# Two blocks, attention with a mixture of experts behind it: where norms, latents and shared pieces stand in the order of the work

## The chip, the cores and the metric

One core of a Trainium2 chip runs the whole program. A core has a matmul engine (TensorE, PE in the profile; its weight loads are shown apart as PEld), a vector engine (VectorE, DVE), a scalar engine (ScalarE, ACT), a general engine (GpSimd, POOL) and a queue engine (SyncE, SP) that issues most of the DMAs. The engines run side by side; each takes its own instructions strictly in the order in which they stand in its queue and waits at a semaphore where an instruction needs something of another engine.

The metric is the time of one execution on the device in microseconds (us), the median of several runs. A second figure is the span of one profiled execution, from its first to its last instruction.

## The reference

Four layers with a residual connection and a layer norm after each: a linear recurrence in place of attention, a quantized gated feed-forward, an attention with latent (low-rank) queries and keys, and a mixture of experts. There are 16 x 256 = 4096 rows of 256 columns, all in fp32. The last two are cut to what matters here:

```python
# second attention, H=16 heads, S=256, causal
cq = rms_norm(x @ w_qa.T, q_a_ln_w)                 # 192 columns
q = (cq @ w_qb.T)                                   # nope 128 + rope 64 per head
ckv = x @ w_kva.T                                   # 64 latent + 64 rope columns
k_pe = rope(ckv[..., 64:]); ckv_l = rms_norm(ckv[..., :64], kv_a_ln_w)
kv = ckv_l @ w_kvb.T                                # k_nope, v per head
attn = softmax(causal(q_full @ k_full.T * 192**-0.5))
x = layernorm(x + (attn @ v) @ w_o.T)
# experts: 32 of them, 4 for each row, at most 160 rows each
topk_idx, topk_w = router(x)
Y = (silu(Xp @ W_gate) * (Xp @ W_up)) @ W_down      # Xp: the rows of each expert
out = zeros.at[slots_token].add(Y * slots_w)
shared = silu(x @ shared_gate.T) * (x @ shared_up.T) @ shared_down.T
x = layernorm(x + out + shared)
```

## The kernel before

The 4096 rows are worked in 8 blocks (b) of 512 rows; a tile holds 128 rows, so a block has 4 tiles (tt). The rows stay on chip in `xs[b]` the whole time. Four stages follow one another: the recurrence (to about 860 us), the feed-forward (to 1126), the second attention (to 1917), and routing, experts and combine (to the end). The change touches the last two.

**Order.** In the second attention the order of PE, DVE, ACT and POOL is the order in which the Python code names the instructions (`manual_schedule`, `engines` are these four). The same holds for the loop over the experts. In the combine only PE's order is written by hand; the compiler plans the rest with a model of time. DMA issues on SP are planned by the compiler throughout.

**Second attention.** The loop over `n` takes one pair of heads of one block in each step: `b, p = divmod(n, 8)`, 64 steps and two before and one behind them. Step n makes, in this order: scores, maxima and exponentials of the first head of pair n+1 (`heads[0]`, L1104, L1115, L1128); the division of the second head of pair n (`divide`, a reciprocal on DVE, L1139, and two products on POOL, L1141); the queries of pair n+2 on PE (L1068 and L1074, two PSUM tiles of tag m, of which there are three); `first_place`; the division of `heads[0]`; the transposes of pair n-1's probabilities for the first sequence and their copies to SBUF by ACT (`keys_first`, a_ps L1154, aT L1158); the turns of the queries of pair n+2 (`turn`, six DVE instructions L1083 to L1085 and two POOL adds L1086); the scores of the second head, `heads[1]`; the contexts of the first sequence (c_ps, L1167, which wait for the copies aT); the transposes and copies for the second sequence; the maxima of `heads[1]`; `second_place`; the exponentials of `heads[1]`; the contexts of the second sequence. Up to three of POOL's row scatters (L1000) of an older block stand in between. The scores have two PSUM buffers (s_ps), which the maxima free.

`first_place` and `second_place` put other work into the steps. `moments` and `normalize` are a block's layer norm: at p = 2 of block b, DVE takes the moments of block b-1 behind its last output projection (o_ps, L1186) and POOL the power -1/2; at p = 3 `first_place` issues one small DVE instruction (shift, L159) and four ACT activations (L162), one for each tile. `step_route` advances the routing of block b-1 (mostly DVE, from p = 3 of block b to p = 1 of the next).

`latents(b)` is a generator of nine pieces that prepare the low-rank queries and keys of a block: the transposed rows (1), four times a product with `w_lat` on PE (lat_ps, L680), its copy and two squares on ACT, the last of them with the rms factors (DVE, then two powers on POOL; 2 to 5), eight scaled ACT copies cq (L704, L705; 6), the key columns kf on DVE (7), the transposed queries cqT (PE and ACT; 8), the transposed keys kT (9). For block b+1 they come at p = 7 of block b-1, then at p = 0, 1, 2, 3, twice in the two places of p = 4 (cq in `first_place`), once more in `second_place` of p = 4, and at p = 5. For block 1 the first piece comes ahead of the loop, the others in the steps of block 0 like all others.

**Experts and combine.** For each of 32 experts, PE transposes its rows (t_ps), multiplies gate and up (gu_ps, L1443) and down (d_ps, L1458); ACT scales the result (ye), and POOL issues two indirect stores of it to `res_d` in DRAM (L1472). `shared_pieces` is a generator of 40 pieces for the shared expert: transposed rows, two halves of gate and up with their silu, two halves of down with their addition to `xs`. 26 of them come ahead of the experts, one behind every eighth turn of the experts' loop (L1496, 4 in all), the last ten in the combine. The combine reads `res_d` back in 16 loads of 1 MB (L1528, nine buffers), each held back until all indirect stores have landed; for each load POOL adds two of the four rows of a token and `xs` (L1536), PE adds the others into PSUM with an identity matrix (y_ps, L1540), DVE adds the two sums (L1547), and behind each second load come moments, power, normalization on ACT (os, L162) and the store of 512 rows (L1514). Behind each load's matmuls `next(parts_, None)` puts one shared piece, and all that are left ahead of the last block.

Of the kernel before, what the change touches and what calls it, by code (L numbers as in the profile page):

```python
# [88 lines left out]
def seq_postln_kernel(ctx: ExitStack, tc: tile.TileContext, a: dict, out: bass.AP, cap: int):  # L89
# [54 lines left out]
    def moments(ys):  # L144

        n = len(ys)
        mv = small.tile([P, n, 2], F32, tag=f"mv{n}", name="mv")
        for i, y in enumerate(ys):
            st = small.tile([P, 6], F32, tag="bn", name="bn")
            nc.vector.bn_stats(st, y)  # L150
            nc.vector.bn_aggr(mv[:, i, :], st)
        rstd = small.tile([P, n], F32, tag=f"rstd{n}", name="rstd")
        rsqrt(rstd, mv[:, :, 1], 1.0, LN_EPS)
        return mv, rstd

    def normalize(ys, dsts, mv, rstd, eng=nc.vector):
        if eng is nc.scalar:
            shift = small.tile([P, len(ys)], F32, tag=f"shift{len(ys)}", name="shift")
            nc.vector.scalar_tensor_tensor(shift, mv[:, :, 0], -1.0, rstd, ALU.mult, ALU.mult)  # L159
        for i, (y, dst) in enumerate(zip(ys, dsts)):  # L160
            if eng is nc.scalar:
                nc.scalar.activation(  # L162
                    dst, y, AF.Identity, bias=shift[:, i : i + 1], scale=rstd[:, i : i + 1]
                )
            else:
                nc.vector.tensor_scalar(
                    dst, y, mv[:, i, 0:1], rstd[:, i : i + 1], ALU.subtract, ALU.mult
                )
# [123 lines left out]
    with ExitStack() as ph:  # L292
# [268 lines left out]
        with tc.manual_schedule(engines=engines):  # L561
# [7 lines left out]
            for m in range(NM + 1):  # L569
                b, p = divmod(m, NPR)  # L570
# [35 lines left out]
                if new:  # L606
# [5 lines left out]
                    if p in (3, 4, 5) and b + 1 < NB:  # L612
                        if p == 3:
                            mixing, xms_next = mixed(xb, nc.gpsimd, nc.gpsimd), {}
                        n, xm = next(mixing)
# [128 lines left out]
    with ExitStack() as ph:  # L744
# [35 lines left out]
        with ExitStack() as ff:  # L780
# [50 lines left out]
            last = None  # L831
            xT = transposed(0, mo_x, ps_t, "t")
            for b in range(NB):
# [9 lines left out]
                last = (b, hT)  # L843
# [30 lines left out]
        return x.unsqueeze(1).to_broadcast([P, K, GT, E])  # L874

    ROUTE_PARTS = 11
    ROUTE_PIECES, PIECES_EARLY, PIECES_STEP = 10, 14, 8
    SH_EARLY = 0
    xTs, dests, scattered = {}, {}, []

# [165 lines left out]
    with ExitStack() as ph:  # L1046
# [101 lines left out]
        def keys_first(heads, s):  # L1148

            aTs = []  # L1150
            for sm in heads:
                a_ps = ps_a.tile([P, 3 * P], F32, tag="a", name="a_ps")
                for i in range(3):
                    nc.tensor.transpose(  # L1154
                        a_ps[:, i * P : (i + 1) * P], sm.pr[:, s, i * P : (i + 1) * P], ident
                    )
                aT = pa.tile([P, 3 * P], F32, tag="aT", name="aT")
                copy = nc.scalar.copy(aT, a_ps)  # L1158
                aTs.append(aT)
            return aTs, copy  # L1160
# [38 lines left out]
        lats, routes, norms, sh_hTs = {}, {}, {}, {}  # L1199
# [8 lines left out]
        def step_latents(b):  # L1208
            if b < NB:
                if b not in lats:  # L1210
                    lats[b] = latents(b, ps_m, "m")
                next(lats[b])

        def step_route(b):
            if b >= 0:
                if b not in routes:
                    routes[b] = route(b, ps_m, "m")
                next(routes[b], None)

        def first_place(b, p):  # L1220
            last = b - 1
            if p == 3 and last >= 0:
                x = x_t[last * NTT : (last + 1) * NTT]
                normalize(x, x, *norms.pop(last), eng=nc.scalar)
            if p == 4:
                step_latents(b + 1)
            if p >= 5:
                step_route(last)
            if p == 0:
                step_route(last - 1)  # L1230

        def second_place(b, p):
            last = b - 1
            if p < 2:
                step_route(last - 1)
            if 3 <= p:
                step_route(last)
            if p == 4:
                step_latents(b + 1)
            if p <= 5 or p == 7:  # L1240
                step_latents(b + 2 if p == 7 else b + 1)
            if p in (1, 2) and last >= 0:
                output(last, 1, p - 1)
                if p == 2:
                    norms[last] = moments(x_t[last * NTT : (last + 1) * NTT])
            if p in (5, 6):
                output(b, 0, p - 5)
            if p == 7:
                shared(last, 0)
            if p == 0:  # L1250
                shared(last - 2, 3)
                shared(last - 1, 1)
            if p == 6:
                shared(last - 1, 2)

        def scatters(b, p):

            lo = 3 * (p - 2)
            return [(b, j) for j in range(max(lo, 0), min(lo + 3, GT * K))] if b >= 0 else []

        NS = NB * NP
        with tc.manual_schedule(engines=engines):
            qTs, sms = {}, {}
            step_latents(1)
            for n in range(-2, NS + 1):
                b, p = divmod(n, NP)
                todo = scatters(b - 2, p)

                def one_scatter():
                    if todo:  # L1270
                        scatter(todo[0][0], [todo.pop(0)[1]])

                scored = n + 1 if 0 <= n + 1 < NS else None
                asked = n + 2 if 0 <= n + 2 < NS else None
                seen = n - 1 if 0 <= n - 1 < NS else None
                if scored is not None:
                    kT = latent[scored // NP][2]
                    heads = sms[scored] = [Softmax(), Softmax()]
                    qT2 = qTs.pop(scored)
                    for s in range(2):  # L1280
                        heads[0].scores(qT2[0], kT, s)
                        heads[0].maxima(s)
                        heads[0].exps(s)
                if n in sms:
                    sms[n][1].divide()
                if asked is not None:
                    q_ps = queries(latent[asked // NP][0], asked % NP)
                if n >= 0:
                    first_place(b, p)
                if scored is not None:  # L1290
                    heads[0].divide()
                if seen is not None:
                    pair = sms.pop(seen)
                    kf = latent[seen // NP][1]
                    part, j = divmod(seen % NP, NP // 2)
                    if j == 0:
                        cT = cTs[seen // NP, part] = pc.tile(
                            [P, NP // 2, BLK], F32, tag="cT", name="cT"
                        )
                    c_ps = ps_c.tile([P, 2, S], F32, tag="c", name="c_ps")  # L1300
                    aTs0 = keys_first(pair, 0)
                if asked is not None:
                    qTs[asked] = [turn(ps, 2 * asked + k) for k, ps in enumerate(q_ps)]
                one_scatter()
                if scored is not None:
                    heads[1].scores(qT2[1], kT, 0)
                    heads[1].scores(qT2[1], kT, 1)
                if seen is not None:
                    contexts(c_ps, *aTs0, kf, 0)
                    aTs1 = keys_first(pair, 1)  # L1310
                if scored is not None:
                    heads[1].maxima(0)
                    heads[1].maxima(1)
                one_scatter()
                if n >= 0:
                    second_place(b, p)
                if scored is not None:
                    heads[1].exps(0)
                    heads[1].exps(1)
                if seen is not None:  # L1320
                    contexts(c_ps, *aTs1, kf, 1)
                    nc.scalar.copy(cT[:, j, :], c_ps.rearrange("p s t -> p (s t)"))
                one_scatter()
            step_route(NB - 2)
            last = NB - 1
            for s in range(2):
                output(last, 1, s)
            x = x_t[last * NTT :]
            layernorm(x, x)
# [26 lines left out]
    with ExitStack() as ph:  # L1356
        ps_t = ph.enter_context(tc.tile_pool(name="ps_t3", bufs=8, space=PSUM))
        sh_psum = ps_t, "t"
        parts_ = shared_pieces()
# [24 lines left out]
    with ExitStack() as ph:  # L1384
# [101 lines left out]
        with tc.manual_schedule(engines=engines):  # L1486
            now = {}
            for n in range(E + 2):
                if n < E:
                    now[n] = Expert(n)  # L1490
                    now[n].turned()
                if 0 <= n - 1 < E:
                    now[n - 1].hidden()
                if 0 <= n - 2:
                    now.pop(n - 2).result()
                if n % PIECES_STEP == PIECES_STEP - 1:  # L1496
                    next(parts_)
    exp.close()

    with ExitStack() as ph:
# [15 lines left out]
        for b in range(NB):  # L1518
# [6 lines left out]
            for pair in range(H):  # L1525
# [8 lines left out]
                n = K - 1 if b == NB - 1 else K - 2  # L1534
# [90 lines left out]
```

## Time and profile before

| | |
|---|---|
| time, median of three runs | 2145.63 us (2143.16 to 2147.37) |
| the profiled execution | 2142.17 us |
| its span | 2140.4 us |
| mean granted PE clock | 0.994 |
| busy PE / DVE / ACT / POOL | 2055.8 / 1560.8 / 763.0 / 899.4 us |
| DMA moved | 169.73 MB, 79 GB/s on average |

By stage (us from the start; busy us of each engine, from windows over the trace):

| stretch | what | PE | DVE | ACT | POOL | DMA share |
|---|---|---|---|---|---|---|
| 0 to 860 | recurrence | 843.3 | 721.9 | 167.0 | 260.7 | 0.44 |
| 860 to 1126 | feed-forward | 266.0 | 74.1 | 54.9 | 11.6 | 0.08 |
| 1126 to 1917 | second attention | 747.8 | 643.9 | 465.0 | 490.3 | 0.03 |
| 1917 to 1981 | routing of the last block, shared pieces | 61.5 | 35.3 | 17.6 | 32.5 | 0.30 |
| 1981 to 2063 | experts | 81.6 | 46.5 | 37.0 | 54.1 | 0.43 |
| 2063 to 2140 | last stores and combine | 55.7 | 39.1 | 21.5 | 50.2 | 0.73 |

How to read it: busy is the time in which an engine worked on an instruction; DMA share is how busy the 16 DMA engines were on average. A timeline line gives start, duration, engine, line, operation, output and inputs by their names in the program, shapes and the number of instructions merged; in brackets stand the idle time of the engine before it and what ended it. The chain of work that ended last is followed back from the last instruction: at each step to what released it, or to the instruction before it on the same engine.

### The profile page before, as it was taken

How to read it: one execution, taken by the hardware profiler on the slowest of the kernel's cores; microseconds unless marked ns; L12 is line 12 of the kernel's file. 1: busy time of each engine (PE TensorE's matmuls, PEld its weight loads, DVE VectorE, ACT ScalarE, POOL GpSimd, SP SyncE). 2: the span in 40 equal slices, each digit the busy share in tenths (PEclk: the TensorE clock that was granted, in tenths of full speed). 3: DMA queues.
4: the chain of work that ended last, by engine and by line, in shares of the span. 5: the costliest groups of instructions: out<-in, count | busy, mean ns of one | idle time of the engine just before them, and what ended most of it. 6: DMA issues, size and time to landing. Idle time of an engine off the chain costs nothing.

```text
span 2140.4 us, 29554 instructions
## 1 busy us (share of the span) xinstructions
PE 2055.8 (96%) x9544; PEld 1439.3 (67%) x9544; DVE 1560.8 (73%) x3960; ACT 763.0 (36%) x2237; POOL 899.4 (42%) x972
## 2 busy tenths in 40 slices
PE   8999999999999999999998999999999999989978
PEld 5777777777777777556564666666666666666866
DVE  7888888888888888232327669797978888875546
ACT  2212121212111111211314665656565655542433
POOL 5622232323232321000004554666576757655576
PEclk9999999999999999999999999999999999999999
DMA  9544444444443220300000000000000000041547
GB/s 314 183 134 146 135 143 132 138 128 138 134 142 120 91 89 29 91 16 20 1 1 1 1 1 1 23 9 4 4 5 2 3 2 3 2 150 51 141 173 270
DMA packets 102042, 169.73 MB, mean 79 GB/s; under 512 B 17807, under 2 KB 67191, under 8 KB 99712
## 3 DMA queue, kind: packets, MB, share of 16 engines
q1 hardware_dynamic: 88000, 158.45, 23.1%
q0 software_dynamic: 9216, 5.19, 0.9%
q10 hardware_dynamic: 4672, 4.21, 0.6%
q8 instruction: 76, 1.25, 0.2%
q14 instruction: 78, 0.64, 0.1%
HBM read 128.75 MB, written 56.95 MB: 87 GB/s over the span
## 4 chain that ended last, share of the span: by engine, by line
PE 74%; DVE 18%; ACT 5%; issue 1%; POOL 1%; DMA 0%; DVEq 0%; POOLq 0%; ACTq 0%; SPq 0%
PE p_ps L419 16%; PE o_ps L512 10%; PE v_ps L449 9%; PE g_ps L208 5%; PE u_ps L208 5%; PE s_ps L1104 4%; PE d_ps L247 3%; PE o_ps L1186 3%; PE c_ps L1167 3%; PE a_ps L1154 3%; PE q_ps L1068 2%; DVE sm L1115 2%; ACT pr L1128 2%; PE gu_ps L1443 2%; DVE eq L862 2%; DVE turned L1085 2%
## 5 line engine op out<-in xcount | busy, mean ns | idle before, releaser
L499 POOL TENSOR_TENSOR wkv<-su,Wr_sb 128x512 f32<-128x512 f32 x128 | 160.0, 1271 | 504.5 <-PE p_ps L419 314.0
L1141 POOL TENSOR_TENSOR pr<-pr,rr 128x256 f32<-128x256 f32 (+1 forms) x256 | 206.9, 835 | 159.6 <-DVE rr L1139 113.6
L1128 ACT ACTIVATE pr<-sm,nm 128x128 f32<-128x128 f32 (+1 forms) x512 | 226.2, 445 | 94.5 <-DVE nm L1115 94.5
L512 PE MATMUL o_ps<-w_o,wkv 128*128 128x256 f32 (+1 forms) x1024 | 251.4, 388 | 7.8 <-POOL wkv L499 7.5
L449 PE MATMUL v_ps<-xm,w_Wv 128*128 128x512 f32 x512 | 242.5, 596 | 6.7 <-DVE xm L395 6.7
L512 PEld LDWEIGHTS o_ps<-w_o,wkv 128*128 128x128 f32 x1024 | 192.2, 190 | 77.2 <-POOL wkv L499 46.4
L1104 PE MATMUL s_ps<-kT,qT 128*128 128x128 f32 (+1 forms) x1024 | 198.3, 337 | 24.1 <-DVE nm L1115 19.8
L421 ACT COPY t_sb<-p_ps 128x256 f32<-128x256 f32 x128 | 47.3, 369 | 466.6 <-PE p_ps L419 465.3
L419 PEld LDWEIGHTS p_ps<-xm,w_Wk 128*128 128x128 f32 x896 | 170.3, 190 | 52.7 <-issue 27.8
L419 PE MATMUL p_ps<-xm,w_Wk 128*128 128x256 f32 x896 | 204.2, 379 | 1.5 <-DVE Wr_sb L424 1.5
L419 PE MATMUL p_ps<-xm,w_Wr 128*128 128x256 f32 x896 | 204.4, 379 | 0.7 <-POOL xm L401 0.5
L1086 POOL TENSOR_TENSOR qT<-qT,turned 128x512 f32<-128x512 f32 x128 | 162.6, 1272 | 87.3 <-DVE turned L1085 87.3
L419 PEld LDWEIGHTS p_ps<-xm,w_Wr 128*128 128x128 f32 x896 | 170.0, 190 | 25.2 <-DVE Wk_sb L424 0.9
L1104 PEld LDWEIGHTS s_ps<-kT,qT 128*128 128x128 f32 x1024 | 146.1, 193 | 45.3 <-issue 31.6
L1158 ACT COPY aT<-a_ps 128x384 f32<-128x384 f32 x256 | 109.7, 480 | 173.1 <-PE a_ps L1154 173.1
L470 DVE TENSOR_TENSOR_SCAN st<-decay,kv 128x255 f32<-128x255 f32 x256 | 163.8, 681 | 4.4
L1115 DVE CUSTOM_DVE_ANT_0 sm<-s_ps,const 128x128 f32<-128x128 f32 (+1 forms) x512 | 154.1, 353 | 15.1 <-PE s_ps L1104 12.5
L142 POOL TENSOR_TENSOR rstd<-rs_t,nhalf 128x4 f32<-128x4 f32 (+1 forms) x33 | 33.3, 1008 | 289.8 <-DVE rs_t L141 279.5
L494 ACT ACTIVATE Wr_sb<-Wr_sb 128x512 f32<-128x512 f32 x128 | 73.5, 621 | 217.6 <-DVE Wr_sb L427 188.6
L1000 POOL DMA_INDIRECT xp_d<-xs,dest x128 | 130.4, 1018 | 46.2 <-issue 31.9
L449 PEld LDWEIGHTS v_ps<-xm,w_Wv 128*128 128x128 f32 x512 | 97.7, 191 | 75.1 <-issue 61.3
L218 DVE TENSOR_TENSOR hT<-sg,u_ps 128x512 f32<-128x512 f32 x56 | 38.4, 686 | 143.7 <-PE u_ps L208 139.3
(189 smaller groups left out, 3737.5 us busy)
## 6 DMA issues: line engine op xcount, KB each, us to landing
w_Wk<-wsum_d SPq DMA_DIRECT2D x56, 448.0 KB, 3.7
w_Wr<-wsum_d SPq DMA_DIRECT2D x56, 448.0 KB, 3.2
w_Wv<-in_Wv_dram SPq DMA_DIRECT2D x64, 256.0 KB, 2.7
res_d<-zeros SPq DMA_DIRECT2D x16, 1024.0 KB, 5.4
res<-res_d SPq DMA_DIRECT2D x16, 1024.0 KB, 11.0
w_e<-in_W_experts_dram SPq DMA_DIRECT2D x32, 384.0 KB, 7.8
xp_d<-empty SPq DMA_DIRECT2D x4, 1360.0 KB, 8.4
xe<-xp_d SPq DMA_DIRECT2D x32, 170.0 KB, 2.6
```

Of the source, the lines that this page charges most:

```text
L208: mm = nc.tensor.matmul(ps, lhsT=w[:, c, i * P : (i + 1) * P], rhs=xT[:, c, :], start=(c == 0), stop=(c == DC - 1),)
L419: nc.tensor.matmul(to, lhsT=w[:, at, :], rhs=x[:, bt, :], start=True, stop=True)
L449: nc.tensor.matmul(ps, lhsT=self.w3["Wv"][:, 2 * h + c, :], rhs=self.xms["Wv"][:, 2 * c : 2 * c + 2, :].rearrange("p s t -> p (s t)"), sta ...
L470: nc.vector.tensor_tensor_scan(st[:, s, 1:], decay[:, n : n + 1].to_broadcast([P, S - 1]), kv[:, s, : S - 1], 0.0, ALU.mult, ALU.add,)
L499: nc.gpsimd.tensor_tensor(wkv, self.su[h], self.both(self.r, h), ALU.mult)
L512: nc.tensor.matmul(ps.rearrange("p t d -> p (t d)") if opens else ps[:, tt % 2, :], lhsT=self.wkv[h][:, tt * P : (tt + 1) * P], rhs=w_o[:, ...
L1000: put = nc.gpsimd.indirect_dma_start(out=xp_d[:, :], out_offset=bass.IndirectOffsetOnAxis(ap=dest[:, k, t : t + 1], axis=0), in_=xs[b][:, ...
L1086: nc.gpsimd.tensor_tensor(qT, qT, qr, ALU.add)
L1104: nc.tensor.matmul(ps[:, lo:hi], lhsT=qT[:, s * S + i * P : s * S + (i + 1) * P], rhs=kT[:, s * S : s * S + hi - lo], start=True, stop=True,)
L1115: nc.vector.tensor_tensor_reduce(out=sm[:, lo:hi], in0=self.ps[s][:, lo:hi], in1=cst["mask"][:, lo:hi], scale=-(DQ**-0.5), scalar=-MASKED, ...
L1128: nc.scalar.activation(self.pr[:, s, lo:hi], self.sm[s][:, lo:hi], AF.Exp, bias=self.nm[:, s, i : i + 1], scale=-1.0, accum_out=self.rs[:, ...
L1141: nc.gpsimd.tensor_tensor(self.pr[:, :, lo:hi], self.pr[:, :, lo:hi], rr[:, :, i : i + 1].to_broadcast([P, 2, hi - lo]), ALU.mult,)
```

## The change

Three edits of order; no instruction is added, removed or changed.

1. `first_place` is split. Its norm (p = 3) and its piece of latents (p = 4) go into a new `middle_place`, which is called behind `keys_first(pair, 0)` and ahead of the turns. The routing steps stay.
2. Block 1's latents: three pieces (the first three products) at step n = -2, two (the fourth product with the rms factors, and the scaled copies) in the second place of n = -1. The three that are left come at p = 0, 1 and 2 of block 0; `next(lats[b], None)` lets the later calls find nothing.
3. Five shared pieces (half of down of block 5, the two halves of gate and up of block 6, the transposed rows of block 7, half of down of block 6) come behind the experts' loop, in its PSUM buffers and its order by hand. The combine has five left.

```diff
-    ROUTE_PIECES, PIECES_EARLY, PIECES_STEP = 10, 14, 8
+    ROUTE_PIECES, PIECES_EARLY, PIECES_STEP, PIECES_LAST = 10, 14, 8, 5
...
-                next(lats[b])
+                next(lats[b], None)
...
         def first_place(b, p):
+            last = b - 1
+            if p >= 5:
+                step_route(last)
+            if p == 0:
+                step_route(last - 1)
+
+        def middle_place(b, p):
+
             last = b - 1
             if p == 3 and last >= 0:
                 x = x_t[last * NTT : (last + 1) * NTT]
                 normalize(x, x, *norms.pop(last), eng=nc.scalar)
             if p == 4:
                 step_latents(b + 1)
-            if p >= 5:
-                step_route(last)
-            if p == 0:
-                step_route(last - 1)
...
                 if n >= 0:
                     first_place(b, p)
+                elif n == -2:
+
+                    for _ in range(3):
+                        step_latents(1)
                 if scored is not None:
                     heads[0].divide()
...
                     aTs0 = keys_first(pair, 0)
+                if n >= 0:
+                    middle_place(b, p)
...
                 if n >= 0:
                     second_place(b, p)
+                elif n == -1:
+                    for _ in range(2):
+                        step_latents(1)
                 if scored is not None:
                     heads[1].exps(0)
                     heads[1].exps(1)
...
                 if n % PIECES_STEP == PIECES_STEP - 1:
                     next(parts_)
+
+            for _ in range(PIECES_LAST):
+                next(parts_)
     exp.close()
```

## The prediction

> **What bounds the kernel now.** I read the page's busy table and 40 slices first: TensorE (PE) is busy 96% of the span, DMA is near its limit only at the very end. Then the chain that ended last:
>
> ```profile
> PE 74%; DVE 18%; ACT 5%; issue 1%; POOL 1%; DMA 0%; DVEq 0%; POOLq 0%; ACTq 0%; SPq 0%
> PE p_ps L419 16%; PE o_ps L512 10%; PE v_ps L449 9%; PE g_ps L208 5%; PE u_ps L208 5%; PE s_ps L1104 4%; PE d_ps L247 3%; PE o_ps L1186 3%; PE c_ps L1167 3%; PE a_ps L1154 3%; PE q_ps L1068 2%; DVE sm L1115 2%; ACT pr L1128 2%; PE gu_ps L1443 2%; DVE eq L862 2%; DVE turned L1085 2%
> ```
>
> Three quarters of the end are set by PE, 18% by VectorE (DVE), 5% by ScalarE (ACT). So an edit pays where the chain leaves PE for another engine or where PE idles. The change touches three such places.
>
> *Second attention.* PE's timeline at b = 1, for an ordinary step (p = 2), then p = 3, then p = 4 (start, duration, idle time before in brackets):
>
> ```profile
> 1258.26 1.48 PE L1104 MATMUL s_ps<-kT,qT 128*128 128x128 f32 x8
> 1259.66 0.87 PE L1167 MATMUL c_ps<-aT,kf 128*64 128x256 f32 x8
> ...
> 1271.60 1.48 PE L1104 MATMUL s_ps<-kT,qT 128*128 128x128 f32 x8
> 1273.85 0.87 PE L1167 MATMUL c_ps<-aT,kf 128*64 128x256 f32 x8 [0.78 <-ACT aT L1158]
> ...
> 1283.21 1.48 PE L1104 MATMUL s_ps<-kT,qT 128*128 128x128 f32 x8
> 1285.92 0.87 PE L1167 MATMUL c_ps<-aT,kf 128*64 128x256 f32 x8 [1.24 <-ACT aT L1158]
> ```
>
> From the second head's scores (s_ps) to the first contexts (c_ps) an ordinary step takes 1259.66 - 1258.26 = 1.40 us, p = 3 takes 2.25, p = 4 takes 2.71. Both long ones wait for ACT's copy aT. What ACT does there at p = 3 (same columns):
>
> ```profile
> 1271.00 2.06 ACT L162 ACTIVATE xs<-xs,shift,rstd 128x256 f32<-128x256 f32 x4
> 1272.97 0.83 ACT L1158 COPY aT<-a_ps 128x384 f32<-128x384 f32 x2
> 1275.24 0.87 ACT L1158 COPY aT<-a_ps 128x384 f32<-128x384 f32 x2 [1.44 <-PE a_ps L1154]
> ```
>
> Four norm activations (L162) run before the copies that PE waits for; the next pair of copies then finds ACT idle for 1.44 us. At p = 4 eight scaled copies cq (L704/L705, 0.29 us each, 2.33 in all) stand in the same place. The same distances, 2.25 and 2.71, come again at 1763.71 and 1775.32.
>
> *The beginning of that attention.* PE's first steps, and the granted clock (last but two column) inside them:
>
> ```profile
> 1132.51 2.08 PE L1104 MATMUL s_ps<-kT,qT 128*128 128x128 f32 x8 [4.27 <-POOL qT L1086]
> ...
> 1143.65 2.88 PE L1104 MATMUL s_ps<-kT,qT 128*128 128x128 f32 x8 [3.58 <-DVE nm L1115]
> ```
>
> ```profile
> 1134.00:1135.00 1.00, 1.00 (x3) 0.64 (x2) 0.70 (x5) 0.98 (x5) 1.00 (x2) 0.50 0.00 0
> ```
>
> After 4.27 and 3.58 us of idleness PE runs 3.3 us at clock 0.50; after the next gap (2.54 us) it stays at 1.00.
>
> *The end.* The chain, then two stretches of the combine (busy time of PE, weight load, DVE, ACT, POOL, clock, DMA share, GB/s):
>
> ```profile
> 2067.50 2.30 DMA res_d<-ye,to
> ...
> 2069.88 4.87 DMA res<-res_d
> ...
> 2074.89 3.75 PE y_ps L1540 x8
> ```
>
> ```profile
> 2071.00:2114.00 43.00, 39.11 (x144) 28.19 (x145) 25.01 (x59) 11.65 (x22) 37.64 (x31) 0.91 1.01 402
> 2074.90:2116.70 41.80, 41.80 (x157) 30.52 (x158) 26.61 (x63) 11.65 (x22) 40.26 (x33) 0.95 1.01 396
> ```
>
> PE idles from its last expert matmul (2062.80) to 2074.89, because the combine waits for POOL's last indirect stores and the load of their rows. Then PE is busy without a gap to 2129.3. But in that time DMA is at a share of 1.01 and 402 GB/s, and POOL is busy 40.26 of 41.80 us: three engines near their limits at once.
>
> **Part A, norms and scaled latents behind the copies.** Nothing is added or removed: 4 ACT activations and one DVE shift (p = 3, b = 1 to 7), 8 ACT copies (p = 4) go behind two aT copies; no DMA and no POOL instruction is moved. At p = 3: exps end at 1271.1, the transposes start at 1270.89 and an ordinary aT starts 0.58 later (1257.55 to 1258.13), so aT runs 1271.47 to 1272.21; c_ps then starts 1.40 after s_ps, at 1273.00. Gain 2.25 - 1.40 = 0.85. The norms fill 1272.21 to 1274.18. Queued behind them are the second copies, whose input comes at 1273.80 + 0.58 = 1274.38, and the transposes of the normed rows on PE at about 1274.5: 0.2 to 0.3 us to spare. The shift now stands behind a reciprocal on DVE, 0.1 us later, before aT ends. At p = 4: gain 2.71 - 1.40 = 1.31; cq ends about 0.16 us after the second copies could start, but the contexts that need them stand behind l_ps and cqT_ps (1.72 + 0.87 us on PE), so nothing waits.
>
> Does the gain survive? From 1289.65 to 1337.2 the chain is DVE (routing, turns, maxima), which idled 1.25 us before 1289.65. Its turns at p = 4 start when ACT's exps end, earlier by p = 3's 0.85; DVE is then free at 1287.55, and PE and ACT deliver at 1287.5. So 2.10 of 2.16 us pass on, and what follows moves with it. Seven times 0.85 (5.95) plus six times 1.31 (7.86; block 0 belongs to part B) less 6 x 0.06 = 13.4. Bounds: 10 if the 0.2 us margins are missed at every block (13 x 0.25 lost), 13.8.
>
> **Part B, block 1's latents at the beginning.** Five pieces move from steps 0 to 4 into steps -2 and -1 (four lat_ps of 1.08 us on PE, 4 x 1.24 of copies and squares on ACT, two DVE and two POOL instructions of rms, eight cq); the later ones (kf, cqT, kT) move up to steps 0 to 2. Steps 1 to 5 now take 9.87, 9.88, 9.88, 11.07, 12.69 = 53.4 (s_ps to s_ps). Without lat and cq, PE needs 8.79 plus cqT 0.87, kT 0.44, and for step 5 3.46 of o_ps. But a step has a DVE floor: s_ps waits for a buffer that is free after queries (4.36), turns (4.28) and one maximum (0.6), about 9.25. So 9.66 + 9.25 x 3 + 12.25 = 49.7, gain 3.7.
>
> The cost: cq stands on ACT ahead of heads[1].exps in step -1 and waits for rms, which waits on DVE behind turns and maxima (to 1143.97) and on POOL for one or two powers of 1.0 us. It ends near 1147 instead of not existing; the exps behind it (1.75, then the next head's 1.77) end 0.5 to 1.5 us later than now, and the reciprocal and the turns of step 0 wait for them (1149.7 now). PE then idles some 7 us and, as after the two gaps above, runs 3.3 us at half clock: 1.7 us. Against it, the lats fill the two first gaps; that clock saving (1.75 and 1.71) is mostly absorbed by the wait for cq. Loss 2.2 to 3.2, and up to 2.0 more if the second and third lat_ps wait for the query buffers (three buffers of tag m, two held until the turns). Best case: loss 0.5. B is +3.7 - 2.5 = +1.2, bounds -1.5 and +3.2.
>
> **Part C, five pieces behind the last expert.** They go from the first five calls of the combine to 2062.80: sh 1.93, four g/u pairs 6.88, xT 0.87, sh 1.73 = 11.4 us of PE. Cover: the idle 12.09 us there; with about 1 us of waiting for two buffers they end near 2075, so the first y_ps is at most 0.4 late. It also finds the clock up (1.73 instead of 3.75). On PE alone the combine would end 11.4 + 2.0 earlier; if the cover were gone the pieces would cost what they save. But POOL needs 30 adds of 1.27 and 7 powers of 1.02 from 2074.92: 2120.2. DMA has 16.78 MB of rows and four or five stores of 0.52 MB to move before the last rows land: 18.9 to 19.4 MB at 402 GB/s from 2071.5 is 2118.5 to 2119.7, and the last pair's matmuls (12 records, 2.6) follow: 2121 to 2122.4. The last DVE add starts at 2129.81 now and 10.6 us follow it. So C gains 7.4 to 9 if release of the nine row buffers (held until ACT's os) keeps pace; if the last rows land as late as now (2120.4), 6.8; if the compiler's new order puts one power and one os (1.02 + 2.08) in the way of the last rows, about 5. I take 7.5. The pieces' own ACT and DVE work (0.60 and 0.69 us each) is beside POOL's last stores, which keep their 1.21 us apart now too while DVE is busy (2053 to 2059); no piece has a POOL or DMA instruction.
>
> [...]
>
> **Sum.** 13.4 + 1.2 + 7.5 = 22.1. The profiled execution took 2142.17 (span 2140.4 and 1.8 around it), 3.5 below the median 2145.63 of the three timed runs, so the same 22.1 taken from each gives 2120.1 for a profile and 2123.5 for the median.
>
> **Rivals.** (1) *The combine stays bound by DMA and POOL*: the five pieces go, but the last rows land when they do now because the nine buffers are released by ACT's os, and SP waited 29.5 us for those. For it: share 1.01. Against it: DMA falls to 0.81 between 2114 and 2120, so it has room. C gives 0 to 1: 2131. (2) *A new wait on ACT takes the old one's place*: the norms end 0.2 us before the second copies and the transposes of the normed rows; if aT starts half a microsecond later than worked out, PE waits there instead and A keeps under half: 2145.6 - 6 - 1.2 - 7.5 = 2131 to 2137 (all of A gone). Against it: the ordinary steps show 2.06 us of ACT idle before the second copies. (3) *Slower*: the moved ACT work is exposed in full. If the second copies were needed at once, each block would lose 1.97 at p = 3 and 2.33 at p = 4 instead of 0.85 and 1.31, 7 x 1.12 + 6 x 1.02 = 14 slower, and with B and C's 8.7 back 2151. It decides when ACT has under 1.4 us between the two pairs of copies; C's timeline line shows 1.44 and PE has 2 us of other work ahead of those contexts. (4) *The edit does little*: part B without A or C is 2144; nothing in the profile speaks for it.
>
> **How the numbers follow.** Forecast 0.66; rival 1 0.13; rival 2 0.12; rival 3 0.06; rival 4 0.03. Forecast's own range: sums of the bounds 10 - 1.5 + 5 = 13.5 and 13.8 + 3.2 + 9 = 26, so 2119.6 to 2132. Rival 1 and the better half of rival 2 lie at its upper end: 2117 to 2133 with the runs' spread of 2 us holds eight in ten. A change under 0.2% (4.3 us) can't be told from none here. Faster 0.91, same 0.03, slower 0.06.
>
> **What would show it.** Right: s_ps to c_ps of 1.40 at p = 3 and 4, and L162 no longer in the chain; a block of 96.5 us instead of 98.6; a gap of about 7 us and half clock before step 1 of the attention; pieces between 2040 and 2055 on PE without a clock drop, last rows and POOL's last add setting the end of the combine. Wrong: c_ps still waiting for aT, xT_ps waiting for L162, or a combine that ends as long after the last indirect store as now (73 us).

## The result, and the profile after

| | before | after |
|---|---|---|
| time, median of six runs | 2147.05 us (2143.16 to 2147.37) | 2155.31 us (2153.05 to 2158.52) |
| ratio to before, 95% interval | 1 | 1.0045 (1.0035 to 1.0056) |
| profiled execution / span | 2142.17 / 2140.4 us | 2157.25 / 2155.5 us |

The kernel is 8.3 us slower by the medians; 2123.5 was forecast. The two profiled executions lie 15.1 us apart, because the one of before was 4.9 us under its median and the one of after 1.9 us over. The stages below add up to the 15.1.

| stage, by the starts of PE's scores and of the first expert's t_ps, and the end of the span | before | after | difference |
|---|---|---|---|
| up to the second attention's first scores | 1132.51 | 1133.10 | +0.6 |
| from there to step p = 0 of block 1 (part B) | 97.53 | 97.91 | +0.4 |
| from there to step p = 5 of block 7, which scores the last pair but one (part A) | 646.61 | 662.83 | +16.2 |
| to the first expert | 104.12 | 103.82 | -0.3 |
| first expert to the end (part C) | 159.6 | 157.8 | -1.8 |

The loss sits in part A. The chain that ended last, shares by engine and then by line, now reads:

```profile
PE 72%; DVE 22%; ACT 3%; issue 2%; POOL 1%; DMA 1%; DVEq 0%; POOLq 0%; ACTq 0%; SPq 0%
PE p_ps L419 16%; PE o_ps L512 10%; PE v_ps L449 9%; PE g_ps L208 4%; PE u_ps L208 4%; PE s_ps L1104 4%; PE d_ps L247 3%; PE o_ps L1186 3%; DVE sm L1115 3%; PE q_ps L1068 2%; PE c_ps L1167 2%; DVE turned L1085 2%; PE a_ps L1154 2%; DVE turned L1084 2%; DVE qT L1083 2%; PE gu_ps L1456 2%
```

DVE went from 18% to 22%, PE from 74% to 72%, ACT from 5% to 3%: ACT did leave the chain, as forecast, and DVE came in. PE's timeline in after shows why. First p = 4 of block 1, then p = 3 of block 2 (start, duration, idle time before):

```profile
1284.17 1.48 PE L1104 MATMUL s_ps<-kT,qT 128*128 128x128 f32 x8
1285.58 0.87 PE L1167 MATMUL c_ps<-aT,kf 128*64 128x256 f32 x8
```

```profile
1369.21 1.48 PE L1104 MATMUL s_ps<-kT,qT 128*128 128x128 f32 x8
1370.62 0.87 PE L1167 MATMUL c_ps<-aT,kf 128*64 128x256 f32 x8
1371.42 0.88 PE L1154 MATMUL a_ps<-const,pr 128*128 128x128 f32 x6
1372.84 0.33 PE L179 MATMUL xT_ps<-const,xs 128*128 128x128 f32 x1 [0.55 <-ACT xs L162]
...
1374.32 0.77 PE L179 MATMUL xT_ps<-const,xs 128*128 128x128 f32 x5 [0.16 <-ACT xs L162]
1376.36 2.49 PE L680 MATMUL lat_ps<-w_lat,xT 128*128 128x320 f32 x4 [1.27 <-DVE turned L1085]
```

From the scores to the contexts it is 1.41 us in both places (1285.58 - 1284.17, 1370.62 - 1369.21), the 1.40 that was forecast. At p = 4 the step, from scores to scores, falls from 12.73 to 11.42 us. But at p = 3 PE idles five times behind that: 0.55 and three times 0.16 for the norms, 1.27 for lat_ps's PSUM buffer, which the turns free. That step took 11.60 us before and takes 15.86 here. DVE in the same step of before, then DVE and POOL in after:

```profile
1367.79 0.17 DVE L1139 RECIPROCAL rr<-rs 128x4 f32<-128x4 f32 x1
1367.94 0.16 DVE L159 SCALAR_TENSOR_TENSOR shift<-mv,rstd 128x4 f32<-128x4 f32 x1
```

```profile
1368.74 0.18 DVE L1139 RECIPROCAL rr<-rs 128x4 f32<-128x4 f32 x1 [1.00 <-ACT pr L1128]
1368.83 3.32 DVE L159 SCALAR_TENSOR_TENSOR shift<-mv,rstd 128x4 f32<-128x4 f32 x1
1372.08 0.68 DVE L1083 TENSOR_TENSOR qT<-q_ps,const 128x512 f32<-128x512 f32 x1
```

```profile
1367.88 1.05 POOL L1000 DMA_INDIRECT xp_d<-xs,dest  x1 [0.20 <-DVE rr L1139]
1368.95 3.18 POOL L1141 TENSOR_TENSOR pr<-pr,rr 128x256 f32<-128x256 f32 x4
1374.31 1.27 POOL L1086 TENSOR_TENSOR qT<-qT,turned 128x512 f32<-128x512 f32 x1 [2.19 <-DVE turned L1085]
```

The shift, 128 x 4 numbers, takes 3.32 us; in before it took 0.16, at 1367.94, behind the first reciprocal and ahead of the second. It now stands behind both reciprocals, which are what POOL's four products wait for; the first two products had also stood behind the scatter (L1000). It begins 0.12 us ahead of the products and ends at 1372.15, 0.02 us behind the last of them (1368.95 + 3.18). The turns behind it start at 1372.08 instead of 1369.06. ACT, which needs the shift for the norms:

```profile
1369.08 0.86 ACT L1158 COPY aT<-a_ps 128x384 f32<-128x384 f32 x2 [0.38 <-PE a_ps L1154]
1372.19 2.07 ACT L162 ACTIVATE xs<-xs,shift,rstd 128x256 f32<-128x256 f32 x4 [2.25 <-DVE shift L159]
1374.17 0.83 ACT L1158 COPY aT<-a_ps 128x384 f32<-128x384 f32 x2
```

ACT sits idle for 2.25 us and then does its norms ahead of the second copies, at 1372.19 instead of 1369.94 (1369.08 + 0.86, where the copies end). All seven shifts of after (minimum, median and maximum in ns):

```profile
L159 DVE SCALAR_TENSOR_TENSOR shift<-mv,rstd x7: 705/3314/3321, 1272.2 to 1875.1; 128x4 f32<-128x4 f32 x7
```

Steps p = 3 of blocks 1 to 7 take 11.61, 15.86, 14.21, 16.05, 16.05, 14.21 and 12.90 us instead of 11.61 (10.53 in block 7): 20.7 lost. In block 1 the shift takes 0.70 us, and the step keeps its old length. In blocks 2, 4 and 5 the same idleness also ends in a drop of the clock: the stretch 1376.40 to 1378.80 runs at 0.50, and lat_ps takes 2.49 us instead of the 1.35 of blocks 3 and 6. The steps p = 4 give back 5.8; in blocks 4 and 5 they take 12.61 and 12.33 instead of 11.42, since they begin at clock 0.50 (1580.67 to 1583.00, 1683.63 to 1686.00).

At the beginning (part B), PE waits 2.84 and 5.29 us, where one gap of about 7 was forecast. Behind both gaps it is slow: the queries take 3.57 and 3.37 us instead of 1.88, and the stretches 1144.30 to 1147.70 and 1155.60 to 1160.00 run at clock 0.50:

```profile
1142.87 1.55 PE L1104 MATMUL s_ps<-kT,qT 128*128 128x128 f32 x8 [2.84 <-DVE nm L1115]
1144.26 3.57 PE L1068 MATMUL q_ps<-cqT,w_q 128*128 128x512 f32 x4
...
1155.69 2.90 PE L1104 MATMUL s_ps<-kT,qT 128*128 128x128 f32 x8 [5.29 <-DVE nm L1115]
1158.38 3.37 PE L1068 MATMUL q_ps<-cqT,w_q 128*128 128x512 f32 x4
```

In the combine (part C) three windows over the trace (length, busy time of PE, weight load, DVE, ACT, POOL, clock, DMA share, GB/s), and then ACT's normalizations:

```profile
2091.90:2116.00 24.10, 23.22 (x85) 16.93 (x86) 10.46 (x28) 3.86 (x7) 20.55 (x17) 0.93 1.01 421
2116.00:2121.00 5.00, 5.00 (x25) 4.41 (x24) 3.83 (x11) 2.08 (x4) 4.92 (x5) 1.00 0.56 159
2121.00:2141.00 20.00, 18.22 (x82) 14.85 (x80) 17.45 (x53) 8.30 (x16) 18.03 (x17) 1.00 0.97 352
```

```profile
2106.72 2.08 ACT L162 ACTIVATE os<-res,shift,rstd 128x256 f32<-128x256 f32 x4 [2.02 <-DVE shift L159]
...
2117.54 2.08 ACT L162 ACTIVATE os<-res,shift,rstd 128x256 f32<-128x256 f32 x4 [7.61 <-DVE shift L159]
```

DMA moves 421 GB/s until 2116, then only 159 for 5 us: a hole. The nine row buffers are free again only when ACT has normalized them, and between the first two such steps lie 10.8 us (2106.72 to 2117.54), 7.61 of them waiting for DVE's shift. The five pieces themselves ran at clock 1.00 (2080.54 to 2091.00), and PE then waited another 2.15 us for the first rows (2091.89): the pieces were covered.

### The profile page after: what moved, and what is told of

Same layout as the page of the kernel before. It is cut to its first block, busy times and chain, and to the rows that moved or that the text cites. A ratio compares the mean times of both kernels' runs of the same rounds, so it can differ in the third digit from the quotient of the medians.

```text
span 2155.5 us, 29587 instructions
## 1 busy us (share of the span) xinstructions
PE 2072.0 (96%) x9544; PEld 1445.1 (67%) x9544; DVE 1581.9 (73%) x3960; ACT 764.8 (35%) x2237; POOL 897.2 (42%) x972
## 4 chain that ended last, share of the span: by engine, by line
PE 72%; DVE 22%; ACT 3%; issue 2%; POOL 1%; DMA 1%; DVEq 0%; POOLq 0%; ACTq 0%; SPq 0%
PE p_ps L419 16%; PE o_ps L512 10%; PE v_ps L449 9%; PE g_ps L208 4%; PE u_ps L208 4%; PE s_ps L1104 4%; PE d_ps L247 3%; PE o_ps L1186 3%; DVE sm L1115 3%; PE q_ps L1068 2%; PE c_ps L1167 2%; DVE turned L1085 2%; PE a_ps L1154 2%; DVE turned L1084 2%; DVE qT L1083 2%; PE gu_ps L1456 2%
## 5 line engine op out<-in xcount | busy, mean ns | idle before, releaser
L1115 DVE CUSTOM_DVE_ANT_0 sm<-s_ps,const 128x128 f32<-128x128 f32 (+1 forms) x512 | 154.1, 353 | 16.7 <-PE s_ps L1104 14.4
L1000 POOL DMA_INDIRECT xp_d<-xs,dest x128 | 127.8, 999 | 46.3 <-issue 32.0
```

What stands on the lines that cost most here:

```text
L1000: put = nc.gpsimd.indirect_dma_start(out=xp_d[:, :], out_offset=bass.IndirectOffsetOnAxis(ap=dest[:, k, t : t + 1], axis=0), in_=xs[b][:, ...
L1115: nc.vector.tensor_tensor_reduce(out=sm[:, lo:hi], in0=self.ps[s][:, lo:hi], in1=cst["mask"][:, lo:hi], scale=-(DQ**-0.5), scalar=-MASKED, ...
```

## The experiments

They ran in three batches on other chips of the same kind, where the kernel before takes 2186 to 2188 us: routing and experts are slower there, while the attention's ordinary steps agree with the traces above to 0.02 us. With B alone, which changes neither, it is 124.2 us from step p = 5 of block 7 to the first expert (104.1 in before), and 106.1 from the experts' first t_ps to their last d_ps (82.6 in before). So each is given as its ratio to before in the same batch; 0.1% is 2.2 us.

**Each part alone.** The diff's hunks for A, for B or for C are kept and the other two undone.

> Part A alone (norms with their shift, and scaled latents, behind the copies); B and C undone. Theory (A holds the whole loss): some 9 to 16 us slower than before, 2156 to 2163, with shifts of 3.3 us. Rival (B's work at the beginning or C's pieces make it slower): within 3 us of before.

> Part B alone (block 1's latents at the beginning). The two traces give a cost of 0.4 us up to the second block; the theory expects before plus 0 to 1 us. Rival (B carries the loss): over 4 us slower.

> Part C alone (five shared pieces behind the last expert). From the first expert to the end the traces give 1.8 us less than before: before minus 1 to 3 us. If the shift's delay also disturbed the combine, the 7.5 us that were forecast would show here: minus 6 or more.

A alone: 1.0051 (1.0034 to 1.0067), 11 us slower; p = 3 takes 14.2 to 15.9 us in blocks 2 to 6, p = 4 11.42 to 11.57. B alone: 0.9995 (0.9985 to 1.0005), nothing that can be told. C alone: 0.9982 (0.9973 to 0.9992), 3.9 us faster, a little more than the 1 to 3 expected of this run. So the loss is A's, and C is worth about half its forecast in the prediction. The three ratios multiply to 1.0028, beside 1.0045 for the whole on the first chip; with the intervals that is no contradiction.

**The shift early.**

```diff
         def first_place(b, p):
             last = b - 1
+            if p == 3 and last >= 0:
+                x = x_t[last * NTT : (last + 1) * NTT]
+                shifts[last] = shifted(x, *norms[last])
...
         def middle_place(b, p):
...
-                normalize(x, x, *norms.pop(last), eng=nc.scalar)
+                normalize(x, x, *norms.pop(last), eng=nc.scalar, shift=shifts.pop(last))
```

> All three parts as in the change, but the shift (the VectorE instruction of 128x4 that the four norms need) is issued where it stood before, ahead of the second reciprocal; only the four activations stay behind the softmax copies. Theory (the shift, with two SBUF inputs, is shut out for 3.3 us while POOL multiplies four softmax blocks, and the turns and norms behind it are late): every shift takes 0.16 us, the step p = 3 takes 10.8 to 11.6 us in blocks 2 to 6 instead of 14.2 to 16.1, p = 4 takes 11.42 in all of them, and the time falls by 15 to 25 us from the changed kernel's 2155: 2130 to 2140, faster than before. Rival (the norms between the two pairs of copies are themselves too late for the transposes and the second copies): p = 3 stays over 13 us and the time at 2150 or above.

0.9934 (0.9917 to 0.9951): 14.4 us faster than before. From after, which is at 1.0045, this kernel differs only in that one instruction of 0.16 us stands one place earlier on DVE. Steps p = 3 take 10.95 us in blocks 1 to 6 and 9.68 in block 7, p = 4 11.42 in all six. PE at p = 3 of block 1:

```profile
1271.86 1.48 PE L1109 MATMUL s_ps<-kT,qT 128*128 128x128 f32 x8
1273.27 0.87 PE L1172 MATMUL c_ps<-aT,kf 128*64 128x256 f32 x8
1274.07 0.87 PE L1159 MATMUL a_ps<-const,pr 128*128 128x128 f32 x6
1274.78 1.04 PE L184 MATMUL xT_ps<-const,xs 128*128 128x128 f32 x8
1275.75 1.34 PE L685 MATMUL lat_ps<-w_lat,xT 128*128 128x320 f32 x4
```

Scores to contexts 1.41, no wait for the norms. The rival (norms themselves too late) falls.

**What the late instruction does, apart from what it computes.** On top of the early shift, one spare instruction behind the copies whose result nobody reads:

```diff
+                spare = small.tile([P, 4], F32, tag="spare", name="spare")
+                nc.vector.scalar_tensor_tensor(spare, mv[:, :, 0], -1.0, rstd, ALU.mult, ALU.mult)
```

and for the second kernel `nc.vector.reciprocal(spare, rstd)` in its place.

> The kernel with the early shift, plus one spare VectorE instruction of the shift's form (128x4, both inputs in SBUF, nothing reads its result) at the place that the change gave the shift. Theory (a VectorE instruction with two SBUF inputs is held for as long as POOL's four products run, and the turns behind it are late): the spare takes 3.3 us in blocks 2 to 7, 0.7 or less in block 1, the step p = 3 takes 13 to 16 us there, and most of the 25 us are lost again: ratio to before 1.000 to 1.006. Rival (the delay hurt only because the four norms waited for the shift): the spare may be as long, but p = 3 stays near 10.95 to 11.6 and the ratio at 0.993 to 0.996.

> The same with the spare instruction replaced by a reciprocal of 128x4, which has one SBUF input. Theory (the second SBUF input is what is shut out): it takes 0.16 to 0.18 us, p = 3 stays at 10.95, ratio 0.993 to 0.994. Rival (any VectorE instruction on SBUF waits behind POOL's products, or one more instruction at this place is itself too much): 3 us and p = 3 over 13 us, as with two inputs.

With two inputs 1.0054 (1.0037 to 1.0071), with one 0.9939 (0.9917 to 0.9962). The spare instruction in each (minimum, median and maximum in ns, of seven):

```profile
L1242 DVE SCALAR_TENSOR_TENSOR spare<-mv,rstd x7: 708/3315/3327, 1271.9 to 1871.5; 128x4 f32<-128x4 f32 x7
```

```profile
L1242 DVE RECIPROCAL spare<-rstd x7: 146/147/149, 1271.2 to 1851.9; 128x4 f32<-128x4 f32 x7
```

DVE with two inputs, block 2:

```profile
1368.48 0.18 DVE L1144 RECIPROCAL rr<-rs 128x4 f32<-128x4 f32 x1 [0.86 <-ACT pr L1133]
1368.58 3.33 DVE L1242 SCALAR_TENSOR_TENSOR spare<-mv,rstd 128x4 f32<-128x4 f32 x1
1371.83 0.68 DVE L1088 TENSOR_TENSOR qT<-q_ps,const 128x512 f32<-128x512 f32 x1
```

The shift is early here (0.16 us, at 1367.45), the norms wait for nothing late; still the turns start at 1371.83 and p = 3 takes 15.79, 15.34, 14.22, 15.66, 14.21 us in blocks 2 to 6, as in after. So the late turns alone make the loss, and the norms' wait adds nothing that shows. With one input p = 3 takes 11.02: its own 0.07. It is neither the place nor one instruction more. The two spares differ in their operation too, but the operation alone does not explain it: among instructions of one operation, TENSOR_TENSOR, the comparisons below, with two inputs in SBUF, are held (up to 1.94 us instead of 0.29), and the turns, with one in PSUM, are not (0.66 to 0.70 us beside the same products, 0.69 to 0.70 where none runs). For these instructions what is left is the second input from SBUF. How POOL's products hold them, these runs do not show.

**The buffers of the combine.** `bufs=9` becomes `bufs=13` for the rows (`res`), on top of the early shift, and alone on the kernel before.

> The kernel with the early shift, and 13 buffers instead of nine for the rows that the combine loads. Theory (with five pieces gone the combine is bound by loads that wait for a buffer, which ScalarE's norms release): the hole in the DMA share near the end of the combine closes and part C's gain rises from 3.6 to about 7 us: 3 to 4 us less than with nine, ratio 0.9915 to 0.992. Rival (POOL's adds and powers, or DMA at 1.0, set the end whatever the buffers): within 1 us of the kernel with the early shift, ratio 0.993 to 0.994.

> The kernel before with 13 row buffers instead of nine and nothing else. Theory (before, PE sets the combine's end and the buffers do not): within 0.1% of before, ratio 0.999 to 1.001. Rival (the buffers bind without the moved pieces too): the 3.2 us that they gave on top of part C, ratio 0.9985.

With C 0.9916 (0.9898 to 0.9933), alone 1.0003 (0.9994 to 1.0013). From the first y_ps to the end it is 65.8 us without C (part B alone), 61.9 with C and nine buffers (early shift), 58.7 with thirteen. Two windows of 10 us in the middle of the combine (columns as above), first with nine buffers, then with thirteen:

```profile
2130.00:2140.00 10.00, 10.00 (x48) 8.81 (x47) 7.95 (x22) 2.08 (x4) 9.36 (x8) 1.00 0.94 335
2140.00:2150.00 10.00, 7.99 (x38) 6.74 (x37) 9.92 (x31) 6.12 (x12) 9.07 (x9) 1.00 0.95 330
```

```profile
2130.00:2140.00 10.00, 10.00 (x48) 8.81 (x47) 8.32 (x22) 2.08 (x4) 9.13 (x8) 1.00 1.02 417
2140.00:2150.00 10.00, 10.00 (x48) 8.81 (x47) 9.93 (x29) 4.15 (x8) 9.38 (x9) 1.00 1.03 409
```

The 335 and 330 GB/s become 417 and 409. Without C the buffers give nothing: PE sets the end there (in before it is busy for all of the 41.80 us from its first y_ps on). The ratios of nine and thirteen have overlapping intervals; the 3.2 us rest on the traces, and these agree: 61.8 to 61.9 us in five kernels with C and nine buffers, 58.7 to 58.9 in three with thirteen.

**Block 1's cq one step later.** The second place of n = -1 makes one `step_latents(1)` instead of two.

> The kernel with the early shift, and of part B's five pieces only four at the beginning: the eight scaled latents cq of block 1 go one step later, behind the first steps' exps. Theory (cq ahead of the second head's exps delays the first steps and takes back what B gains): from the first scores to block 1's first step 2 to 3 us less than the 97.75 of the early shift; ratio 0.992 to 0.993. Rival (the beginning is bound by VectorE's floor of 9.55 us a step and by the gaps before the first steps, whichever way): within 0.7 us.

0.9925 (0.9908 to 0.9942). Block 1's first step starts at 1228.96, 1229.96 and 1227.37 us in the three kernels with this edit, and at 1229.99 to 1232.97 in the five that have A and B without it: 2.2 us less on average (1228.8 and 1231.0), with a scatter of 1.5 from the stages ahead. From the first scores, as the expectation counts it, that is 93.4, 96.5 and 95.2 us beside 96.8 to 97.9. The 2 to 3 expected are not contradicted, but not settled either: the interval holds the ratio of the early shift.

**All together.**

> The early shift, cq one step later and 13 row buffers together; nothing else differs from the changed kernel. If the three gains add (ratios 0.9934, about 0.9985 and 0.9982 of what each came on top of), the ratio to before is 0.990, some 21 us faster. If the combine, begun earlier, is bound by something else, 0.991 to 0.993.

0.9892 (0.9877 to 0.9906), some 22 to 24 us faster than before: the three gains add.

**The same trap in the kernel before.** If two SBUF inputs are what matters, other instructions must suffer without any change. The routing's comparison eq, always 128 x 128, in before's second attention (minimum, median, maximum in ns, between 1240 and 1880 us), and one of them with POOL beside it:

```profile
L862 DVE TENSOR_TENSOR eq<-left,top x24: 292/507/1936, 1306.7 to 1820.0; 128x128 f32<-128x128 f32 x24
```

```profile
1416.47 0.17 DVE L1139 RECIPROCAL rr<-rs 128x4 f32<-128x4 f32 x1
1416.56 0.26 DVE L948 TENSOR_REDUCE top<-left 128x4 f32<-128x128 f32 x1
1416.85 1.93 DVE L862 TENSOR_TENSOR eq<-left,top 128x128 f32<-128x128 f32 x1
```

```profile
1417.00 1.62 POOL L1141 TENSOR_TENSOR pr<-pr,rr 128x256 f32<-128x256 f32 x2
```

It takes 0.29 us when alone, 0.73 where it begins while the first of POOL's two products runs, and 1.93 where it begins just ahead of both: 1.64 more, beside products of 1.62. The slow ones stand behind the division of the second head. The edit moves that division behind the routing:

```diff
-                if n in sms:
-                    sms[n][1].divide()
...
                 if n >= 0:
                     first_place(b, p)
...
+                if n in sms:
+                    sms[n][1].divide()
                 if scored is not None:
                     heads[0].divide()
```

> The kernel before with that one edit alone (divisions behind the routing). Theory: 7 to 14 us faster, ratio 0.9935 to 0.997, with every eq of 128x128 at 0.29 us. Rival: within 0.1% of before, or slower.

> The same, and the two softmax divisions (reciprocal on VectorE, four products on POOL) moved behind the routing's VectorE instructions in every step. Theory of the second SBUF input: the routing's comparisons of 128x128 (eq), which take 0.29 us alone and up to 1.93 us where POOL multiplies, stand in the same trap in the kernel before; ahead of the divisions they take 0.29 everywhere, VectorE is free some 16 us earlier in all, of which 7 to 14 reach the end: ratio 0.984 to 0.987. Rival (the products, now later on POOL, are late for the transposes, or the comparisons are slow for another reason): 0.990 or above, or eq still over 0.7 us.

Alone 0.9935 (0.9917 to 0.9953), 14 us; on top of all together 0.9821 (0.9808 to 0.9835), 39 us faster than before, a little beyond the 0.984 to 0.987 expected, and the fastest of the study. Every one of these eq takes 0.29 us in the kernel with this edit alone:

```profile
L862 DVE TENSOR_TENSOR eq<-left,top x24: 291/292/293, 1308.2 to 1809.7; 128x128 f32<-128x128 f32 x24
```

In the last kernel the step p = 7 of blocks 1 to 6 takes 9.55 to 9.68 us (before, 10.6 in block 1 and 11.2 to 11.4 in the others), and p = 0 behind it 10.25 to 10.38 instead of 10.83 to 11.28.

## Why the prediction was wrong

The step that failed is in part A: "The shift now stands behind a reciprocal on DVE, 0.1 us later, before aT ends." What was costed is the instruction's place in DVE's queue, at the duration it had in its old place. At the new place it takes 3.3 us in six blocks of seven, because POOL's four products run all that time (3.18 us), and what waits behind it on DVE, the turns, hold two of the three PSUM buffers that PE needs. The prediction named what queues behind the norms on ACT, but not what queues behind the shift on DVE. It was also worked out on block 1 alone, the block in which the shift takes only 0.70 us; blocks 2 to 7 have a row scatter ahead of the products, which makes all four run behind the shift's start. The row to look at was in the trace of before: eq of one shape between 0.29 and 1.94 us, behind another reciprocal.

The other steps, one by one:

- *p = 4, gain 1.31*: right to the hundredth (12.73 to 11.42) wherever p = 3 does not leave a low clock behind (0.50, in blocks 4 and 5).
- *p = 3, gain 0.85*: with the early shift 0.66 in blocks 1 to 6 and 0.85 in block 7. Scores to contexts did fall to 1.41; 0.2 went in front of lat_ps and the contexts behind it.
- *2.10 of 2.16 pass on at each block*: too much. With the early shift p = 7 is 0.47 to 0.51 longer in blocks 2 to 6, which fits DVE setting the pace there without having begun that much earlier (no run tests this by itself). From p = 0 of block 1 to p = 5 of block 7 it took 637.3 us (1867.64 - 1230.30) instead of 646.6: 9.3 of the 13.4 forecast. With eq no longer beside POOL's products the loss at p = 7 is gone (9.55 to 9.68 us).
- *Part B, +1.2 (-1.5 to 3.2)*: 0.4 lost in after, inside the bounds; gain and cost cancel. The step ahead of p = 0 fell from 11.14 to 9.78, p = 2 to 4 to 9.55 (forecast 9.25) and p = 5 to 12.26 (12.25). But p = 0 rose from 11.12 to 12.82 and p = 1 from 9.86 to 12.45, where 9.66 was forecast: clock 0.50 came behind both gaps (2.84 and 5.29 us), not one. That cq ahead of the exps costs some 2 (forecast 2.2 to 3.2) fits the runs and is not settled by them.
- *Part C, 7.5 (5 to 9)*: mis-sized. The condition "if release of the nine row buffers keeps pace" did not hold: 1.8 in the first trace, 3.9 alone, 7.1 with thirteen buffers (65.8 - 58.7). The cause that rival 1 gives, loads held back by the buffers' release, is what the runs show; its price of 0 to 1 is too low. The idle time that covers the pieces was 11.07 us and not 12.09: 2062.80 is where the chain leaves PE, whose last d_ps ends at 2063.82.
- *Rivals 2 and 3*: at p = 3, xT_ps waits for L162, the sign of rival 2, but ACT was not too slow: it waited for DVE (2.25 us in block 2). Rival 3's 2151 is near the 2155 measured by luck: its mechanism did not occur.

With that one instruction back in its place the change comes to 0.9934, some 14 us of the 22 forecast; what is missing is in C's buffers, in A's steps p = 3 and p = 7, and in B's first steps.

## What to carry to other kernels

When an instruction moves, ask what runs on the other engines beside it at the new place and how long its like takes beside that work, not only who stands ahead of it. In these traces one shape with a wide spread of durations (0.16 or 3.3 us, 0.29 or 1.93) named the VectorE instructions that were held while POOL worked. Here it paid to put those with two SBUF inputs where they are through before POOL's products start, ahead of the instruction that sets these going: the shift takes 0.16 us there, eq 0.29. The early shift stands behind a reciprocal too, the first: at that place in before, POOL's products begin 0.23 us after it does in block 1, and it is through in 0.16; in the others a scatter comes first. And a gain on a chain that a pool of buffers feeds needs the release times of those buffers worked out, or more buffers.

## What had not been expected of the hardware

- The length of the wait goes with the moment at which the VectorE instruction begins. In the attention's loop, from block 1 on, the 14 traces hold 87 shifts, spares with two SBUF inputs and comparisons eq that begin while a product runs: they take 0.70 to 0.73 us and end 0.02 to 0.15 us behind that one product. Another 78 begin 0.11 to 0.16 us ahead of the first product, by the profile: they are held to the end of the whole run, 1.92 to 1.95 us for two products and 3.31 to 3.33 for four. All others take 0.32 us at most. The shift of block 1 is of the first kind (it begins 0.92 us after the first product and waits for the second), those of blocks 2 to 7 are of the second. Why those that begin early are held through all the products is open, and behind the last scores a few comparisons do not follow this: in after one begins at 1917.47, 0.65 us ahead of two products, and takes 0.77.
- An instruction with one SBUF input was held too: in the combine of before, rs_t (TENSOR_SCALAR, 128x4) takes 1.13 us at 2084.13 and ends 0.02 us behind one of POOL's additions; where none runs it takes 0.16 to 0.17.
- The turns of the queries, with one input in PSUM and one in SBUF, take 0.66 to 0.70 us beside the same products and 0.69 to 0.70 where none runs: they are not held.
- The granted clock fell to 0.50 after gaps of 0.55, three of 0.16 and one of 1.27 us in blocks 2, 4 and 5, and after practically the same gaps in blocks 3 and 6 lat_ps kept its 1.35 us. What decides between the two is open.
